# Batch 0's gate and up projections as seven block products, with the sums of the weights partly made one slot earlier

## The chip, the cores and the metric

The kernel runs on one core of a Trainium2 chip. The metric is the device time of one execution in microseconds. TensorE (PE) multiplies matrices, VectorE (DVE), ScalarE (ACT) and GpSimd (POOL) do the elementwise work, and SyncE (SP) issues most of the transfers (DMAs). Each engine works through its own list of instructions in order; an instruction that waits holds up everything behind it on that engine.

## The reference, cut to what matters

The kernel computes one transformer layer in float32 on 4 batches of 512 rows of 512 numbers, with 32 query heads, 8 key heads and 1376 columns in the feed-forward part:

```python
x = x + attention(layernorm(x), Wq, Wk, Wv, Wo)     # causal softmax, rotary embedding
h = layernorm(x)
x = x + (silu(h @ Wg.T) * (h @ Wu.T)) @ Wd.T        # Wg, Wu: 1376 x 512
```

The change concerns h @ Wg.T and h @ Wu.T of batch 0 only.

## The kernel before

**Slots.** The order of all instructions is written out by hand. After an opening (batch 0's projections) come four slots, one for each batch's attention (`slot`, L1243). A slot runs 8 groups of heads. A group has four "visits", each of which puts scores on PE (L993, L1006), their exponentials on ACT (L1094), the minima on DVE (L1039) and causal selects on POOL (L1099); a group ends with the products with the values, `averages` (L1121). The scores of a group are those of the group two further on, so they run ahead. Between the visits, `gap(n)` first takes some steps from the queue `idle` of extra POOL work (`pool_steps`, L284) and then fills PE with steps of other work in proportion to their stated costs (`fill`). Slot 0 fills with the projections of batches 1 to 3; slot 1 with the last of batch 3's projection, batch 0's output projection (`attended(0)`) and its feed-forward part; slots 2 and 3 and the tail with those of batches 1 to 3.

**Gate and up, the ordinary way.** `ordinary(0)` (L544) goes through 10 blocks of 128 columns of Wg and Wu. For each it adds up four products of a 128x128 block of weights with 512 columns of h. `load_f` fetches the weights (512 KB for a block of both matrices) two blocks ahead, in three buffers of `shared`. ACT makes a tanh (L558), DVE two multiplications (L559, L561). `edge(0)` does the last 96 columns. On the trace every product appears as 8 records, because each is issued in four strips of 32 columns of weights and each strip leaves two records.

**Gate and up, as seven.** Batches 1 to 3 use `seven` (L684). It treats a 256-column piece of Wg or Wu as 2 x 2 blocks, and h as 2 x 2 blocks, and makes the product from seven block products in place of eight, with sums of blocks before and after (a form of Strassen's method). A "unit" is one such piece: 10 units, even ones of Wg, odd ones of Wu. Its seven steps are a1, y1, y2, v1, v2, w1, w2; each is a product of a 256x128 block of weights with 256 columns, that is two products of 128x128 weights with 256 columns. ACT copies one product (L727), DVE joins them (L738, L748, L749, L757), and after an even unit come two tanh (L717) and two DVE steps (L718), after an odd one two multiplications on POOL (L721). The sums of h (`sums_of`, L682) are made once per batch on DVE.

**Sums of the weights.** The seven blocks of each unit lie in DRAM, `packed[u]`. Raw blocks are copied there in slot 0 (`copies`, L653 and L654). Four sums of blocks per unit are made by `packs(u)`: a load of 2 x 256 KB into a spare buffer (L176, half of `xnTs[1]`), four sums on POOL (`combine`, L640) and a store of 512 KB (L643). All 40 sums are made in slot 1. `load_blocks` (L675) loads the blocks of a unit one unit ahead, from `packed`, in the kinds a (128 KB), y, v and w (256 KB each); y, v and w have two buffers, a has one.

**Other transfers in slot 1.** `spilled` (L1303) stores a tile of 2816 KB (`homes[3]`, the memory of `wd_sb`) to DRAM from ACT's queue; `load_down` then loads the down weights there (2560 KB at once), and `load_rest` the last 96 columns of Wg and Wu. `timed` places these at stated points on the axis of the layer's costs. Query rows for the scores are moved by DMAs too: the minima to `lowest` (L1080), and `qa` from `lowest` (five issues, L1089 and L1091, in every group). The transposed, normalised rows of batch 0 (xn) are made partly by DVE (L314) with transfers through a `flip` buffer (L318 to DRAM, L320 back), and for two of four tiles by PE with an identity (L304); the norm's power is a step on POOL (L221), the normalising one on DVE (L226).

Of the kernel before, what the change touches and what calls it, by code (L numbers as in the profile page):

```python
# [18 lines left out]
B, T, D = 4, 512, 512  # L19
NH, NKV, DH = 32, 8, 16  # L20
FF = 1376
P = 128
NT = T // P
NK = D // P
NF = (FF + P - 1) // P
# [49 lines left out]
def preln_block_kernel(  # L75
# [13 lines left out]
    nc = tc.nc  # L89
# [74 lines left out]
    packed = [dram.tile([P, 7, 2 * P], F32, name=f"packed{u}") for u in range(whole)]  # L164
    turn = xnTs[1].rearrange("p k t -> p (k t)")
    sums = turn.rearrange("p (s k t) -> p s k t", s=4, k=2)
    spare = turn.rearrange("p (u f m) -> p u f m", u=2, f=4)
    rest_w = rope_sb[:, : 2 * NK * 96].rearrange("p (a k m) -> p a k m", a=2, k=NK)


# [4 lines left out]
    def load_w(t, src):  # L175
        nc.sync.dma_start(out=t, in_=src.rearrange("(k p) m -> p k m", p=P))  # L176
# [16 lines left out]


    rows = [const.tile([P, 2, D], F32, name=f"rows{n}") for n in range(3)] + [homes[3][:, 8:10, :]]
    ROWS = {0: (0, 1), 1: (2, 0), 2: (1, 3), 3: (2, 0)}
    xr = {(b, i): rows[ROWS[b][i // 2]][:, i % 2, :] for b in range(B) for i in range(NT)}

# [83 lines left out]
    idle = deque()  # L282

    def pool_steps(n):  # L284
        for _ in range(min(n, len(idle))):
            idle.popleft()[1]()

    def need(tag):
        while any(t == tag for t, _ in idle):
# [329 lines left out]
    def after(step):  # L619
        return 0.0, step  # L620

    def packs(u):


        w, at = (wg, wu)[u % 2], 2 * P * (u // 2)
        t = spare[:, u % 2]

        def load():
            for i in range(2):
                load_w(t[:, 2 * i : 2 * i + 2, :].rearrange("p f (k m) -> p (f k) m", k=2), w[:, at + P - P * i :][:, :P])  # L630

        def combine(n):
            a11, a12, a21, a22 = (t[:, f, :] for f in range(4))
            out_, one, two, op = (
                (a22, a21, a22, ALU.add),
                (a21, a11, a21, ALU.subtract),
                (a11, a22, a11, ALU.subtract),
                (a12, a12, a11, ALU.subtract),
            )[n]
            nc.gpsimd.tensor_tensor(out_, one, two, op)  # L640

        def store():
            nc.sync.dma_start(out=packed[u][:, 3:, :], in_=t)  # L643

        return load, combine, store
# [15 lines left out]
    places = {"v": (0, (5, 6)), "w": (1024, (2, 4)), "y": (2048, (1, 3)), "a": (3072, (0,))}  # L661

    def place(kind, v):
        start, blocks = places[kind]
        size = 2 * P * len(blocks)
        return flat[:, start + (size * (v % 2) if kind != "a" else 0) :][:, :size].rearrange(
            "p (f k m) -> p f k m", f=len(blocks), k=2
        )

    def load_blocks(kind, v):  # L670
        if v >= (B - 1) * whole:
            return
        blocks = places[kind][1]
        src = packed[v % whole][:, blocks[0] : blocks[-1] + 1 : max(blocks[-1] - blocks[0], 1), :]
        nc.sync.dma_start(out=place(kind, v).rearrange("p f k m -> p f (k m)"), in_=src)  # L675

    def sums_of(which):
        x = xnTs[0]
        b11, b12, b21, b22 = (x[:, 2 * j : 2 * j + 2, 2 * P * h : 2 * P * h + 2 * P] for j in range(2) for h in range(2))
        t1, t2, t3, t4 = (sums[:, n] for n in range(4))  # L680
        one, two, by = ((t1, b12, b11), (t2, b22, t1), (t3, b22, b12), (t4, b21, t2))[which]
        nc.vector.tensor_tensor(one, two, by, ALU.subtract)  # L682

    def seven(b, n, blocks):  # L684


        x, home = xnTs[0], homes[n]
        rights = (x[:, 0:2, 0 : 2 * P], x[:, 2:4, 0 : 2 * P], x[:, 2:4, 2 * P :], *(sums[:, s] for s in (3, 0, 1, 2)))
        once = rope_sb[:, 2 * NK * 96 : 2 * T]
        carried = deque()  # L690

# [4 lines left out]
        def product(ps, right, w):  # L696
            for k in range(2):
                product_of(ps, w[:, k, :], rights[right - 1][:, k, :], k == 0, k == 1)

        def halved(t):  # L700
            return t.rearrange("p (h t) -> p h t", h=2)

        def unit(u):
            v, a, f = (b - 1) * whole + u, u % 2, 2 * (u // 2)
            left, right = slice(0, 2 * P), slice(2 * P, T)
            out = (u_sb if a else home[:, f : f + 2, :]).rearrange("p f t -> p (f t)")
            corners = out.rearrange("p (h t) -> p h t", h=4)[:, 0:4:3, :]
            ps = {}

            def twice(t):  # L710
                return t.unsqueeze(1).broadcast_to([P, 2, 2 * P])

            def ended():
                for which in (1, 0):
                    g, t = home[:, f + which, :], u_sb[:, which, :]
                    if a == 0:
                        nc.scalar.activation(t, g, AF.Tanh, scale=0.5)  # L717
                        carried.append(lambda g=g, t=t: nc.vector.scalar_tensor_tensor(g, t, 1.0, g, ALU.add, ALU.mult))  # L718
                    else:
                        engine = nc.gpsimd if narrow[0] else nc.vector  # L720
                        engine.tensor_tensor(g, g, t, ALU.mult)  # L721

            def a1():
                load_blocks("y", v + 1)
                ps["a"] = bank()
                product(ps["a"][:, left], 1, place("a", v)[:, 0])
                nc.scalar.copy(once, ps["a"][:, left])  # L727

            def y1():
                load_blocks("v", v + 1)  # L730
                load_blocks("a", v + 1)
                ps["y"] = bank()
                product(ps["y"][:, left], 2, place("y", v)[:, 0])
                owed()

            def y2():
                product(ps["y"][:, right], 6, place("y", v)[:, 1])
                nc.vector.tensor_tensor(halved(out[:, T:]), halved(ps["y"]), twice(once), ALU.add)  # L738

            def v1():  # L740
                load_blocks("w", v + 1)
                ps["v"] = bank()
                product(ps["v"][:, left], 7, place("v", v)[:, 0])
                owed()

            def v2():
                product(ps["v"][:, right], 5, place("v", v)[:, 1])
                nc.vector.tensor_tensor(corners, halved(ps["v"]), twice(out[:, 3 * T // 2 :]), ALU.add)  # L748
                nc.vector.tensor_tensor(out[:, right], ps["v"][:, right], out[:, left], ALU.add)  # L749

            def w1():
                ps["w"] = bank()
                product(ps["w"][:, left], 4, place("w", v)[:, 0])

            def w2():
                product(ps["w"][:, right], 3, place("w", v)[:, 1])
                nc.vector.tensor_tensor(corners, halved(ps["w"]), corners, ALU.add)  # L757
                ended()

            return [(0.86, step) for step in (a1, y1, y2, v1, v2, w1, w2)]  # L760

        steps = []
        for u in range(whole):
            steps += unit(u)
            if u % 2:
                steps.append(after(lambda p=u // 2: later_sums(b, n, p, (0, 1))))
        t = [after(lambda s=s: sums_of(s)) for s in range(4)]
        ends = edge(n)
        steps[12:12] = [after(moved)]
        for cut, step in zip((44, 50, 56, 62, 66, 72), blocks):  # L770
            steps.insert(cut, after(step))
# [407 lines left out]
    begin1[1]()  # L1179
    load_w(wv_sb, wv)  # L1180
    load_columns(wq_sb, wq, P, D)
    load_w(wo_sb, wo)
    thin[0] = False
    for cost, step in turned:
        step()
# [53 lines left out]
    def slot(b, steps):  # L1239
# [19 lines left out]
        def gap(n):  # L1259
            nonlocal done, part  # L1260
            part += total * shares[n] / 8
            pool_steps((3, 2, 2, 0, 3)[n])
            done = fill(steps, part, done)

        for g in groups:
# [36 lines left out]
    def spilled():  # L1302
        nc.scalar.dma_start(out=spill, in_=homes[3])  # L1303

    def load_down():
        whole = FF // P
        load_w(wd_sb[:, :whole, :], wd[: whole * P, :])
        nc.sync.dma_start(out=wd_sb[: FF - whole * P, whole, :], in_=wd[whole * P :, :])

    def restored():  # L1310
        nc.scalar.dma_start(out=homes[1], in_=spill)
# [2 lines left out]
    early = [*rest1[16:-8], *turns, begin3, *rest2, *turned3, *rest3[:-24]]  # L1314
    for u in range(whole):
        early.insert(4 * u + 4, after(lambda u=u: copies(u)))
    slot(0, early)

    before, behind = attended(0, by_pe=(2, 3))
    tiles = list(down(0, 0))  # L1320
# [13 lines left out]
        assert not asides  # L1334
        return out_steps

    asides = []
    for u in range(whole):
        load, combine, store = packs(u)
        at = 8.2 * u + 6.0  # L1340
        asides += [(max(at - 9.9, 0.5), load), (at + 5.0, store)]
        asides += [(at + 1.0 * n, lambda n=n, combine=combine: combine(n)) for n in range(4)]
    asides += [(6.0, spilled), (34.0, load_down), (34.1, load_rest)]
    start1 = [
        before[0],
        *rest3[-24:-12],
        *before[1:],
        after(lambda: load_f(0)),
        *rest3[-12:-1],
        *behind,  # L1350
        rest3[-1],
        after(lambda: load_f(1)),
    ]
    blocks = [after(lambda kind=kind: load_blocks(kind, 0)) for kind in "ayvw"]
    layer = [*ordinary(0), *edge(0), *tiles[:5], *blocks, *tiles[5:cut]]
    slot(1, [*start1, *timed(layer, asides)])

    def split(b, n):

# [65 lines left out]
```

## Time and profile before

| | |
|---|---|
| median of 3 runs | 847.34 us (846.66 to 848.84) |
| the profiled execution | 848.06 us |
| its span in the trace | 845.8 us |
| PE busy | 822.5 us (97%) |
| DVE, ACT, POOL busy | 545.5, 231.3, 352.5 us |
| PE's granted clock | 1.0 in all 40 slices |
| slot 0, from first to last group's averages | 62.1 to 171.1 us |
| slot 1 | 191.4 to 352.7 us |
| slot 2 | 375.2 to 531.1 us |

The span is the time between the first and the last instruction that the profile shows; the execution's own time contains what lies around it. In a row of the timeline the first number is the start of the instruction in the span, the second its length, and "[1.46 <-DMA shared<-in_wg]" behind it tells how long the engine stood idle before it and what released it. A row of a window gives the busy time of each engine in that stretch.

### The profile page before, as it was taken

To read this page: it belongs to the slowest core of one execution; us is meant where nothing else is said; L and a number is where in the kernel's file an instruction comes from. 1 tells how busy PE (TensorE), PEld (TensorE's weight loads), DVE (VectorE), ACT (ScalarE), POOL (GpSimd) and SP (SyncE) were. 2 spreads that over 40 slices of the span, in tenths; PEclk is the share of its full clock that TensorE was granted. 3 is DMA by queue.
4 is the path that set the end of the run, shared out by engine and by line. 5 is a ranking of instruction groups with operands and counts; after the bars stand their busy time and mean duration, and the time that the engine had idled before them with its cause. 6 is when DMAs were issued, how large, how long until landed. Compare 5 with 4: busy or idle time off the path is not lost.

```text
span 845.8 us, 28256 instructions
## 1 busy us (share of the span) xinstructions
PE 822.5 (97%) x11980; PEld 452.2 (53%) x11980; DVE 545.5 (65%) x1601; ACT 231.3 (27%) x342; POOL 352.5 (42%) x514
## 2 busy tenths in 40 slices
PE   6999999999999999999999999999999999999998
PEld 5654444544333335333555555436655556788887
DVE  7877777778555554458677776686877633656632
ACT  1045654422232322222233232222323331011100
POOL 4575574773544344223265634532244444101130
PEclk9999999999999999999999999999999999999999
DMA  8533304003764742253344632325333534545811
GB/s 259 124 96 78 91 16 91 5 3 64 232 191 144 235 137 77 88 200 77 84 155 140 196 115 66 115 47 151 96 97 103 162 106 148 119 146 174 291 33 50
DMA packets 149517, 101.57 MB, mean 120 GB/s; under 512 B 59696, under 2 KB 137264, under 8 KB 149136
## 3 DMA queue, kind: packets, MB, share of 16 engines
q1 hardware_dynamic: 149104, 94.01, 38.3%
q10 hardware_dynamic: 288, 5.77, 1.8%
q8 instruction: 94, 1.54, 0.8%
q14 instruction: 31, 0.25, 0.1%
HBM read 78.32 MB, written 25.17 MB: 122 GB/s over the span
## 4 chain that ended last, share of the span: by engine, by line
PE 76%; DVE 12%; POOL 4%; DMA 3%; issue 2%; ACT 1%; SPq 1%; POOLq 0%; DVEq 0%; ACTq 0%
PE mm L299 38%; PE mm L296 14%; PE sc L993 12%; DVE junk L1039 6%; PE av L1121 6%; PE sc L1006 4%; PE mm L590 2%; POOL e L1099 1%; DMA shared<-packed 1%; PE mm L582 1%; DVE st L218 1%; DVE rot L358 1%; ACT e L1094 1%; POOL home L425 1%; POOL qa L978 1%
## 5 line engine op out<-in xcount | busy, mean ns | idle before, releaser
L1039 DVE CUSTOM_DVE_ANT_0 junk<-sc,mask 128x128 f32<-128x128 f32 (+3 forms) x512 | 251.2, 491 | 139.0 <-PE sc L1006 78.4
L1094 ACT ACTIVATE e<-sc 128x1024 f32<-128x1024 f32 (+1 forms) x192 | 165.5, 882 | 384.4 <-PE sc L1006 300.7
L299 PE MATMUL mm<-xnT,shared 128*32 128x256 f32 (+1 forms) x3520 | 244.2, 420 | 2.3 <-DMA shared<-in_wg 1.5
L1099 POOL TENSOR_SCALAR_AFFINE_SELECT e<-e 128x512 f32<-128x512 f32 (+2 forms) x192 | 105.7, 560 | 225.4 <-ACT e L1094 222.3
L299 PEld LDWEIGHTS mm<-xnT,shared 128*32 128x32 f32 x3520 | 116.9, 110 | 113.0 <-issue 62.8
L993 PE MATMUL sc<-home,qa 32*64 32x512 f32 (+6 forms) x2048 | 156.1, 421 | 6.5 <-DVE low L1039 3.0
L1006 PE MATMUL sc<-qa,home 32*64 32x512 f32 (+6 forms) x2048 | 152.2, 427 | 1.5 <-DVE low L1039 0.8
L993 PEld LDWEIGHTS sc<-home,qa 32*64 32x64 f32 x2048 | 66.8, 131 | 90.2 <-DVE low L1039 29.1
L1121 PE MATMUL av<-e,home 128*32 128x512 f32 (+3 forms) x1024 | 81.9, 438 | 1.8 <-POOL e L1099 1.6
L296 PE MATMUL mm<-xnT,shared 128*128 128x256 f32 x360 | 80.3, 383 | 1.0 <-DMA shared<-packed 1.0
L296 PEld LDWEIGHTS mm<-xnT,shared 128*128 128x128 f32 x360 | 68.3, 192 | 12.8 <-issue 2.2
L299 PE MATMUL mm<-wd_sb,home 128*32 128x256 f32 (+3 forms) x848 | 71.4, 470 | 0.0
L1006 PEld LDWEIGHTS sc<-qa,home 32*64 32x64 f32 x2048 | 58.8, 130 | 22.5 <-issue 8.7
L1121 PEld LDWEIGHTS av<-e,home 128*32 128x32 f32 x1024 | 30.5, 109 | 47.2 <-issue 35.0
L299 PEld LDWEIGHTS mm<-wd_sb,home 128*32 128x32 f32 (+1 forms) x848 | 28.2, 110 | 36.9 <-issue 28.2
L299 PE MATMUL mm<-wo_sb,cx 128*32 128x512 f32 x384 | 45.4, 595 | 0.0
L797 POOL TENSOR_TENSOR wd_sb<-home 128x256 f32<-128x256 f32 x15 | 11.4, 759 | 75.6 <-DVE home L721 75.3
L1039 DVE DVE_READ_ACCUMULATOR2_ANT low<- 128x1 f32 x512 | 42.4, 83 | 0.0
L221 POOL TENSOR_TENSOR rstd<-rstd,neghalf 128x1 f32<-128x1 f32 x24 | 16.0, 667 | 56.8 <-DVE rstd L220 56.7
L1145 POOL TENSOR_TENSOR inv<-us,inverse 128x256 f32<-128x256 f32 x32 | 20.9, 654 | 44.5 <-DVE inverse L1138 44.3
L359 POOL TENSOR_TENSOR rot<-rot,rope_sb 128x512 f32<-128x512 f32 x18 | 25.7, 1425 | 23.0 <-DVE rot L358 22.8
L721 POOL TENSOR_TENSOR home<-home,u 128x512 f32<-128x512 f32 x20 | 25.2, 1281 | 21.2 <-DVE u L757 21.2
(146 smaller groups left out, 855.6 us busy)
## 6 DMA issues: line engine op xcount, KB each, us to landing
shared<-packed SPq DMA_DIRECT2D x90, 256.0 KB
flip<-u SPq DMA_DIRECT2D x88, 64.0 KB
packed<-xnT SPq DMA_DIRECT2D x10, 512.0 KB
xnT<-flip SPq DMA_DIRECT2D x18, 256.0 KB
wd_sb<-differences SPq DMA_DIRECT2D x7, 640.0 KB
shared<-packed SPq DMA_DIRECT2D x30, 128.0 KB
rows<-in_x SPq DMA_DIRECT2D x14, 256.0 KB
out<-rows SPq DMA_DIRECT2D x13, 256.0 KB
```

What stands on the lines that cost most here:

```text
L296: nc.tensor.matmul(out, lhsT=lhsT, rhs=rhs, start=start, stop=stop)
L299: nc.tensor.matmul(out[c : c + 32], lhsT=lhsT[:, c : c + 32], rhs=rhs, start=start, stop=stop)
L359: put(lambda: engine.tensor_tensor(rot, rot, sin, ALU.mult))
L590: nc.tensor.matmul(ps[96:P, ts(q, P)], lhsT=rest_w[:, a, kq, 32 * q : 32 * q + 32], rhs=xnTs[0][:, kq, most:], start=kq == 0, stop=kq == N ...
L721: engine.tensor_tensor(g, g, t, ALU.mult)
L993: nc.tensor.matmul(dst[at : at + 64, :n], lhsT=qa[g][rows_of(r), q : q + 64], rhs=keys_of(g)[rows_of(r), :n], start=True, stop=True,)
L1006: nc.tensor.matmul(dst[at : at + 64, first_q:], lhsT=keys_of(g)[rows_of(r), k : k + 64], rhs=qa[g][rows_of(r), P * j + first_q :], start=True,
L1039: nc.vector.tensor_tensor_reduce(out=junk[:, :n], in0=src, in1=mask[:, T - n : T] if i else mask[:, T:], scale=-1.0, scalar=BIG, op0=ALU.a ...
L1094: nc.scalar.activation(dst, src, AF.Exp, scale=1.0 / math.sqrt(DH))
L1099: nc.gpsimd.affine_select(out=e[rows, heads, c : c + P], in_=e[rows, heads, c : c + P], compare_op=ALU.is_ge, fill=0.0, base=base, pattern ...
L1121: nc.tensor.matmul(av[32 * r : 32 * r + 32, P * j :], lhsT=v[:, j, 4 * (m // 2) + r, DH * (1 - hf) : DH * (3 - hf)], rhs=e[:, r, c : c + n ...
L1145: nc.gpsimd.tensor_tensor(us[m][:, :, hf, :], turned[0][:, :, hf, :], by, ALU.mult)
```

## The change

1. Batch 0 uses `seven(0, 0, ())` in place of `ordinary(0)`; the loads of `load_f` go. The first unit runs in another order: a1, y1, w2, y2, v1, v2, w1. Its sums of h lie in other memory (two in `rows[2]`, two in `xnTs[1]`).
2. The blocks "v" and "w" of the first unit are loaded into two free rows of `homes[0]`; all four kinds of that unit are loaded near the start of slot 1.
3. The sums of the weights are a queue (`idle`) that `gap` works off: packs 0 to 2 (12 sums) in slot 0, with the memory of the output weights `wo_sb` as buffer, and packs 3 to 9 in slot 1, with rows 6 to 9 of `homes[0]`. The loads and stores of packs stand in the same queue and are issued as soon as they come to its head. The load of the output weights moves from before the opening to behind pack 2's store.
4. The down weights are loaded as 11 pieces of 256 KB, spread over the layer, and not at once.
5. The numbers of POOL steps per gap become (1, 1, 0, 0, 0) in slot 0 and (2, 2, 1, 0, 2) in slot 1.

```diff
-    spare = turn.rearrange("p (u f m) -> p u f m", u=2, f=4)
+    sums = [sums[:, n] for n in range(4)]
+    spares = (wo_sb.rearrange("p k t -> p (k t)"), homes[0][:, 6:10, :].rearrange("p f t -> p (f t)"))
+    spares = [t.rearrange("p (u f m) -> p u f m", u=2, f=4) for t in spares]
...
     def pool_steps(n):
-        for _ in range(min(n, len(idle))):
-            idle.popleft()[1]()
+        while idle and (n > 0 or idle[0][0] == "load"):
+            tag, step = idle.popleft()
+            n -= tag != "load"
+            step()
...
     def place(kind, v):
+        if v == 0 and kind in "vw":
+            return homes[0][:, 2 + (kind == "w"), :].rearrange("p (f k m) -> p f k m", f=2, k=2)
...
-            v, a, f = (b - 1) * whole + u, u % 2, 2 * (u // 2)
+            v, a, f = b * whole + u, u % 2, 2 * (u // 2)
...
-            return [(0.86, step) for step in (a1, y1, y2, v1, v2, w1, w2)]
+            order = (a1, y1, y2, v1, v2, w1, w2) if v else (a1, y1, first_w2, y2, v1, v2, last_w1)
+            return [(0.86, step) for step in order]
...
-    load_w(wo_sb, wo)
...
-            pool_steps((3, 2, 2, 0, 3)[n])
+            pool_steps(((1, 1, 0, 0, 0), (2, 2, 1, 0, 2), *[(3, 2, 2, 0, 3)] * 2)[b][n])
...
-    def load_down():
-        whole = FF // P
-        load_w(wd_sb[:, :whole, :], wd[: whole * P, :])
-        nc.sync.dma_start(out=wd_sb[: FF - whole * P, whole, :], in_=wd[whole * P :, :])
+    def load_down(f):
+        rows_of_f = min(P, FF - f * P)
+        nc.sync.dma_start(out=wd_sb[:rows_of_f, f, :], in_=wd[f * P : f * P + rows_of_f, :])
...
+    def pack(us):
+        made = [packs(u) for u in us]
+        idle.extend(("load", load) for load, _, _ in made[:2])
+        for at, (_, combine, _) in enumerate(made):
+            for n in range(4):
+                idle.append(("sum", lambda n=n, combine=combine: combine(n)))
+                if at and n == 2:
+                    idle.append(("load", made[at - 1][2]))
+                if at and n == 3 and at + 1 < len(made):
+                    idle.append(("load", made[at + 1][0]))
+        idle.append(("sum", lambda: None))
+        idle.append(("load", made[-1][2]))
+
+    def pack_first():
+        pack(range(3))
+        idle.append(("sum", lambda: None))
+        idle.append(("load", lambda: load_w(wo_sb, wo)))
...
+    early.insert(4, after(pack_first))
+    slot(0, [*early, after(ready_out)])
...
-    asides = []
-    for u in range(whole):
-        load, combine, store = packs(u)
-        at = 8.2 * u + 6.0
-        asides += [(max(at - 9.9, 0.5), load), (at + 5.0, store)]
-        asides += [(at + 1.0 * n, lambda n=n, combine=combine: combine(n)) for n in range(4)]
-    asides += [(6.0, spilled), (34.0, load_down), (34.1, load_rest)]
+    blocks = [after(lambda kind=kind: load_blocks(kind, 0)) for kind in "ayvw"]
+    layer, first_sums = seven(0, 0, ())
     start1 = [
         before[0],
+        *blocks[:2],
+        after(lambda: pack(range(3, whole))),
         *rest3[-24:-12],
+        *blocks[2:],
         *before[1:],
-        after(lambda: load_f(0)),
-        *rest3[-12:-1],
+        *rest3[-12:-2],
         *behind,
+        rest3[-2],
+        first_sums[0],
         rest3[-1],
-        after(lambda: load_f(1)),
+        first_sums[1],
     ]
-    blocks = [after(lambda kind=kind: load_blocks(kind, 0)) for kind in "ayvw"]
-    layer = [*ordinary(0), *edge(0), *tiles[:5], *blocks, *tiles[5:cut]]
-    slot(1, [*start1, *timed(layer, asides)])
+    asides = [(6.0, spilled), (34.0, load_rest)]
+    asides += [(20.0 + 4.5 * f, lambda f=f: load_down(f)) for f in range(NF)]
+    slot(1, [*start1, *timed([*layer, *tiles[:cut]], asides)])
```

## The prediction, made before the result was known

> **What bounds the kernel now.** I read the page's busy times first, then the windows of each slot, then PE's, POOL's and SP's rows around the start of slot 1, where nearly everything changes.
>
> ```profile
> PE 822.5 (97%) x11980; PEld 452.2 (53%) x11980; DVE 545.5 (65%) x1601; ACT 231.3 (27%) x342; POOL 352.5 (42%) x514
> ```
>
> TensorE is busy for 822.5 of 845.8 us. The windows (PE, PEld, DVE, ACT, POOL busy, granted clock, DMA share, GB/s) say where it is not. The first row below lies in slot 0, the next two in slot 1, the last in slot 2:
>
> ```profile
> 62.00:126.00 64.00, 60.69 (x1146) 28.98 (x1136) 45.56 (x164) 38.44 (x67) 40.61 (x63) 1.00 0.24 62
> 191.00:239.00 48.00, 46.32 (x649) 17.94 (x641) 31.75 (x100) 12.15 (x16) 19.61 (x28) 1.00 0.56 162
> 239.00:284.00 45.00, 45.00 (x608) 15.86 (x601) 24.82 (x80) 13.27 (x17) 20.13 (x32) 1.00 0.65 190
> 420.00:463.00 43.00, 43.00 (x839) 24.70 (x836) 33.71 (x95) 12.99 (x19) 26.32 (x36) 1.00 0.46 146
> ```
>
> Slot 1 has no idle PE beyond 1.7 us in its first window, and the clock is 1.00 throughout. So each product less in slot 1 ends the kernel earlier by its whole length, and each wait that reaches PE's queue there is paid whole.
>
> **Gain 1: fewer columns on PE.** PE's rows in slot 1 (start, length):
>
> ```profile
> 205.97 3.66 PE L299 MATMUL mm<-xnT,shared 128*32 128x256 f32 x64
> 210.51 1.09 PE L304 MATMUL mm<-ident,xn 128*128 128x128 f32 x8
> 213.63 1.92 PE L299 MATMUL mm<-xnT,shared 128*32 128x512 f32 x16 [1.46 <-DMA shared<-in_wg]
> ```
>
> A product of 128x128 weights leaves 8 records. The 64 records with 256 columns are 8 products; the next work starts at 209.56, 3.59 us on, so 0.45 us each. In the chain of the end, 32 records with 512 columns (4 products) take 3.57 to 3.59 us: the same time per column. Cleared of the start of a fill (1.85 us for two, 3.57 for four), 512 columns cost 0.86 us and 256 cost 0.43. Batch 0 has 80 products of 512 now (640 records), and 10 units x 7 x 2 = 140 of 256 then: 160 halves against 140. Saved: 20 x 0.43 = **8.6 us** (9.0 with 0.45).
>
> **Gain 2.** The third row waits 1.46 us for the first ordinary weights, issued only at 208.71. Unit 0's blocks are loaded at the slot's start, some 30 us earlier: **1.5 us** more. Gains: 10.1 us.
>
> **At nothing.** DVE in slot 1 loses 20 gate and up steps (0.687 and 0.688, 13.8 us) and gets per unit 0.69 + 0.69 + 0.425 + 0.69 (24.9 in all), 10 gates of 0.762 and 4 sums (3.0): +21.7 us over 184, or 5.3 us per window of 45. That makes 30 where 24.8 stand; slot 2 runs at 33.7 in 43 with PE full. ACT: 10 copies of 0.364 and 10 of 0.622 for 10 of 0.597, 3.9 us more, against 13 busy of 45. POOL in slot 1: 12 sums of 0.731 out (8.8), 10 multiplies of 1.281 in (12.8). Cover gone, slot 2 shows the price: its PE idle, 1.8 us, is about that of slot 1 (1.9). So 0 to 1. In slot 0 the 12 sums fall into POOL's idle (23 of 64 us in the first row), at one or two a gap: 0, at most 2. The output weights' load goes from SP's start to behind pack 2's store. In the trace the four flips queued after it land 6 to 6.7 us after issue, where later ones need 2.0; but the chain goes through the next flips, at 23.6. Nothing, at best -1.
>
> **What is added: waits at the head of a queue.** The change makes three queues hold things that PE wants soon.
>
> *(a) First group of slot 1 (averages at 191.4).* Pack 3's load stands on SP behind five query rows (ending 179.9) and two block loads, so issues near 181 to 182. A pair of such loads takes 3.4 us alone (issued 251.05, complete 254.8) and up to 5.2 beside others. POOL, free at 182.5, now has two of pack 3's sums ahead of the rotations, and stands until about 185.5. Sums (1.5), rotations (2.6), a third sum (0.7) and the norm's power (0.55) then put the selects of L1099 at 191 to 193 where they ended at 190.5; averages want them near 192.3. 0 to 2 us; I take 1.2.
>
> *(b) Second group (averages at 216.4).* POOL's queue gets pack 5's first sum **ahead of** the power L221 of xn tile 3. In the trace POOL and SP do this there:
>
> ```profile
> 205.92 0.78 POOL L221 TENSOR_TENSOR rstd<-rstd,neghalf 128x1 f32<-128x1 f32 x1 [2.04 <-DVE rstd L220]
> 206.65 2.02 SPq L320 DMA_DIRECT2D xnT<-flip  x2
> 208.71 0.51 SPq L176 DMA_DIRECT2D shared<-in_wg  x1
> 209.27 1.59 SPq L176 DMA_DIRECT2D shared<-in_wu  x1
> ```
>
> Pack 5's load takes the place of the row at 208.71: behind pack 3's store, eight flips and the two L320. Landing 3.4 to 5 us on, it is there at 212.5 to 214.5. Sum 0.73, power 0.78, normalising L226 0.55: xn is ready at 214.5 to 216.5, and PE transposes it (L304) at 210.51 now. L226 also stands ahead of the next minima on DVE, so PE has nothing else. 3 to 5 us if the order holds; below that only if the load is early, so 0 to 5. I take 4.2.
>
> *(c)* DVE gets three sums (0.76 each) ahead of the next group's first minima: 0 to 1, I take 0.5.
>
> *(d) First units.* Count from the first fill after those averages (218.6 before). PE: three steps of 0.86, a visit of scores (1.0), four steps, a visit, then w1 and at **8.0** the next unit's a1. SP: minima at 0.5, pack 4's store, pack 6's load, which waits until that store has landed (stores of 512 KB: 2.6 to 3.1 us alone) so goes at 4.0 to 5.0; then the second unit's y, v and a at 5.0 to 6.5, behind 512 KB. Their latency is 2.9 to 3.2 us alone; a is there at 9.5 to 10. 0 to 2.5; I take 1.8.
>
> *(e) The spill.* It is a 2816 KB store on ACT's queue, after unit 0's two tanh: at about 10.8. SP is then at five query rows (to 9.2), a block load, pack 5's store (10.2), then waits about 3 us for its landing before pack 7's load: at 13.5. The third unit's y, v, a follow at 14.5 to 16, **behind the spill**. Now:
>
> ```profile
> 223.61 0.34 ACTq L1303 DMA_DIRECT2D spill<-wd_sb  x1
> ```
> ```profile
> 223.81 1.00 SPq L176 DMA_DIRECT2D xnT<-in_wu  x2
> 224.85 1.33 SPq L176 DMA_DIRECT2D shared<-in_wg  x1
> 226.29 5.37 SPq L176 DMA_DIRECT2D shared<-in_wu  x1
> 231.76 2.51 SPq L643 DMA_DIRECT2D packed<-xnT  x1
> ```
>
> The trace has the spill complete at 234.5, 10.9 us on, and the loads issued 0.2 to 2.7 us after it complete at 235.2, 236.1, 236.9 and 237.6: none before it. SP itself hung for 5.37 us where an issue takes 0.5. That cost PE nothing, because ordinary weights were loaded two row blocks ahead. Blocks come one unit ahead. So a lands after 10.8 + 10.9 = 21.7, with 896 KB of pack and blocks in front of or beside it: 24 to 26. PE wants it at 16.1, moved by (d) to 18: 6 to 8 us, 0 if SP is past before the spill, 9 with SP held. I take 6.5.
>
> The Trainium skill ("DMA: Bandwidth & Descriptors", Queues, rings and completion order) speaks against (e): each DMA engine takes turns between the queues that have work, a packet at a time. By that rule the blocks would share the engines with the spill and land some 3 us later than alone, not 9, and the sum would be about 5 us lower. The rows above do not show it, so the sum does without it.
>
> *Later units* run as in slot 2, whose same steps wait 0.5 us for blocks; the down weights now come as 256 KB pieces. 0 to 1.
>
> **Sum.** Waits 1.2 + 4.2 + 0.5 + 1.8 + 6.5 = 14.2; gains 10.1; net +4.1. The profiled execution took 848.06 us (span 845.8), so 852.2; the median of the three runs, 847.34, lies 0.7 lower: **851.5 us**. With every wait at its upper end (19.5): 856.7. With all at nothing: 837.2.
>
> **Rivals.**
> *A, not slower: the spill catches no block.* Place: the third unit's a, decided by whether SP issues it before about 10.8 us into that fill. For it: pack 5's store may need no wait if it starts earlier. Against: SP stands behind the minima and two landings. Price: 6.5 less, 845.0.
> *B, POOL is not held.* Pack 5's load would have to land before 205.9; against it stand eight flips and two L320 that end at 208.7. 4.2 less: 847.3.
> *C, both, and the small waits at half:* 10.1 - 1.8 = 8.3 gained, 839.0. What speaks for it is that SP is now idle for long stretches, 180 to 194 among them, and PE's stalls themselves give transfers time.
> *D, more:* POOL, held by pack 7's load, brings the selects late in the next groups too, beyond 857.5.
> *That fewer columns do not save time* has the equal rates per column against it.
>
> **Chances.** Forecast case 0.48 (847.5 to 857.5), A 0.14, B 0.10, C 0.22, D 0.06. This kernel's measurement tells about 0.3% (2.5 us) from no change. Faster: C and half of A, some of the forecast's low end, 0.30; same: B and the rest of A, 0.16; slower: 0.54. The range 839.5 to 857.5 leaves out D and about half of C. The forecast's own range is 847.5 to 857.5.
>
> **What would show it.** Right: PE waits of some microseconds before the transposes L304 with L221 late behind a sum of L640 that waits for DMA; a PE wait for shared<-packed of over 5 us in the third group of slot 1, with blocks landing after the spill; PE's busy time 8 to 9 us lower. Wrong: PE idle in slot 1 near 2 us, as now; blocks that land during the spill; or a wait in slot 0, which I priced at nothing.

## The result, and the profile after

The changed kernel takes 861.52 us (median of five runs, 856.99 to 863.50), the kernel before 848.41 (five runs, 846.66 to 851.78): 1.014 times as long, with a 95% interval of 1.010 to 1.018. It is slower, as forecast, but by 13 us and not by 4, and above the range.

Lines have moved in the changed kernel: products are L304 (L299 before), the transposes L309, POOL's sums L645, the selects L1120, block loads L682, loads of packs L178, their stores L648, the spill L1323. Its page has, in answer to the rows of before:

```profile
PE 819.3 (96%) x12460; PEld 470.9 (55%) x12460; DVE 567.0 (66%) x1635; ACT 233.6 (27%) x352; POOL 366.9 (43%) x524
```
```profile
PEclk9999999999889999999999999999999999999999
```

The profiled execution took 856.99 us (span 855.3). PE is busy only 3.2 us less, not 8.6, and idle 12.7 us more. And two slices, both in slot 1, have a granted clock under nine tenths, which no slice had before. The starts of the groups' averages place the loss: 191.6 for the first of slot 1 (191.4 before), 220.8 (216.4), 254.8 (239.7), and from then on the changed kernel gains: the first of slot 2 is at 385.9 (375.2), and the distance stays. So 15 us are lost in two groups, and 4 come back. PE's waits from 191 to 400 us (total, times, longest):

```profile
PE mm L304 <- DMA shared<-packed: 8.9, 2, 7.2
PE mm L309 <- DVE xn L229: 5.5, 1, 5.5
```

**The wait for the transposes** is the one that step (b) named. POOL and PE (start, length, idle time before):

```profile
214.20 0.72 POOL L645 TENSOR_TENSOR home<-home 128x256 f32<-128x256 f32 x1 [10.93 <-DMA home<-in_wu]
214.88 0.55 POOL L224 TENSOR_TENSOR rstd<-rstd,neghalf 128x1 f32<-128x1 f32 x1
```
```profile
216.54 1.09 PE L309 MATMUL mm<-ident,xn 128*128 128x128 f32 x4 [5.51 <-DVE xn L229]
```

POOL stands 10.93 us at pack 5's first sum, with the power L224 behind it, which took place at 205.92 before; PE pays 5.51 of it.

**The waits for blocks** are steps (d) and (e). The spill goes out between pack 5's store and pack 7's load:

```profile
235.18 0.35 ACTq L1323 DMA_DIRECT2D spill<-wd_sb  x1
```
```profile
233.84 0.70 SPq L648 DMA_DIRECT2D packed<-home  x1
238.02 1.81 SPq L178 DMA_DIRECT2D home<-in_wu  x2
239.93 12.15 SPq L682 DMA_DIRECT2D shared<-packed  x7
```
```profile
234.20 1.07 PE L304 MATMUL mm<-xnT,shared 128*32 128x256 f32 x16 [1.79 <-DMA shared<-packed]
249.76 3.64 PE L304 MATMUL mm<-xnT,shared 128*32 128x256 f32 x32 [7.15 <-DMA shared<-packed]
```

SP comes to pack 7's load at 238.02, because that waits for the store before it to land, and to the third unit's blocks at 239.93. The trace has the spill complete at 246.1 and these blocks at 248.6, 249.3 and 249.6.

**What no step named** is in the last row's length: 32 records of 256 columns are four products and take 1.9 us elsewhere; here 3.64. The windows around both waits (the third number from the right is the granted clock):

```profile
216.00:220.00 4.00, 3.46 (x36) 1.84 (x44) 3.86 (x13) 0.00 (x0) 2.90 (x4) 0.50 0.00 0
220.00:225.00 5.00, 5.00 (x98) 3.41 (x86) 4.66 (x15) 1.23 (x3) 4.79 (x8) 0.96 0.01 3
250.00:254.00 4.00, 4.00 (x48) 1.97 (x48) 0.00 (x0) 0.37 (x1) 2.99 (x3) 0.50 0.16 47
254.00:258.00 4.00, 4.00 (x80) 2.45 (x68) 2.10 (x10) 1.09 (x2) 1.49 (x3) 0.93 0.02 4
```

By the clock record of the trace, PE ran at half its clock from 213.61 to 220.44 us and from 247.75 to 254.57: the clock fell while PE waited, 2.6 and 5.1 us after it had stopped, and came back 3.9 and 4.8 us after it had started again. Half of PE's time at the half clock is 1.95 and 2.41 us.

The Trainium skill has this rule ("TensorE: Matmul & The Clock Gate", What's actually happening): the clock halves after an idle window of about 3.4 us and returns after a busy one of that length, windows that run freely. The half clock and the windows are in the traces: in all fourteen executions kept here, every recorded change of the clock lies a whole number of times 3.41 us behind the first one (above 6.83, 27.31 and 6.82 us apart, which is 2, 8 and 2 windows). How idle a window must be differs from the rule. Short of the kernel's last microseconds the clock fell 15 times in these executions. It fell at the end of every window at full clock in which PE was busy for 36% of the time or less, PE being fully idle in only five of these fourteen; of those with PE busy for 43% or more it fell in one, with 48%. It came back behind windows with 89% or more. So the place of a wait in the windows matters as much as its length: waits of 1.8, 2.6 and 3.1 us were followed by a fall, and others of 1.8, 2.0 and 3.3 were not.

### The profile page after: what moved, and what is told of

Read it like the earlier page. It is cut to its first block, busy times and chain, and to the rows that moved or that the text cites. A ratio compares the mean times of both kernels' runs of the same rounds, so it can differ in the third digit from the quotient of the medians.

```text
span 855.3 us, 29332 instructions
## 1 busy us (share of the span) xinstructions
PE 819.3 (96%) x12460; PEld 470.9 (55%) x12460; DVE 567.0 (66%) x1635; ACT 233.6 (27%) x352; POOL 366.9 (43%) x524
## 4 chain that ended last, share of the span: by engine, by line
PE 74%; DVE 12%; DMA 5%; issue 3%; POOL 3%; SPq 2%; ACT 1%; POOLq 0%; DVEq 0%; ACTq 0%
PE mm L304 35%; PE mm L301 15%; PE sc L1014 11%; DVE junk L1060 6%; PE av L1142 6%; PE sc L1027 4%; PE mm L595 2%; DMA shared<-packed 2%; POOL e L1120 1%; PE mm L587 1%; DVE rot L363 1%; DVE st L221 1%; ACT e L1115 1%; PE mm L309 1%; DMA xa<-in_x 1%
## 5 line engine op out<-in xcount | busy, mean ns | idle before, releaser
L304 PE MATMUL mm<-xnT,shared 128*32 128x256 f32 x3632 | 219.7, 384 | 9.5 <-DMA shared<-packed 9.5
L1120 POOL TENSOR_SCALAR_AFFINE_SELECT e<-e 128x512 f32<-128x512 f32 (+2 forms) x192 | 106.1, 562 | 198.5 <-ACT e L1115 195.4
L304 PEld LDWEIGHTS mm<-xnT,shared 128*32 128x32 f32 x3632 | 122.1, 110 | 97.1 <-issue 33.9
L304 PE MATMUL mm<-wd_sb,home 128*32 128x256 f32 (+3 forms) x848 | 71.2, 470 | 0.0
L728 POOL TENSOR_TENSOR home<-home,u 128x512 f32<-128x512 f32 x30 | 37.8, 1283 | 28.0 <-DVE u L775 27.9
L304 PEld LDWEIGHTS mm<-wd_sb,home 128*32 128x32 f32 (+1 forms) x848 | 28.0, 110 | 36.9 <-issue 27.6
L304 PE MATMUL mm<-wo_sb,cx 128*32 128x512 f32 x384 | 45.4, 595 | 0.0
L724 ACT ACTIVATE u<-home 128x512 f32<-128x512 f32 x40 | 23.0, 622 | 63.0 <-DVE home L775 53.8
L645 POOL TENSOR_TENSOR home<-home 128x256 f32<-128x256 f32 x28 | 21.4, 765 | 35.9 <-DMA home<-in_wu 26.5
```

The lines of the kernel that those rows point to most:

```text
L304: nc.tensor.matmul(out[c : c + 32], lhsT=lhsT[:, c : c + 32], rhs=rhs, start=start, stop=stop)
L1120: nc.gpsimd.affine_select(out=e[rows, heads, c : c + P], in_=e[rows, heads, c : c + P], compare_op=ALU.is_ge, fill=0.0, base=base, pattern ...
```

## The experiments

Theory 1: the two long waits of slot 1 are what the prediction says they are, and each is longer by the half clock behind it. The rivals: the clock falls for another reason; there is simply too much to transfer in that stretch; the waits move elsewhere when one is removed. The kernel before was measured anew beside each group of runs: 848.00 us beside the first four below, 848.25 beside those on wait (b), on blocks ahead and on five and six packs, 848.14 beside the two with a third buffer, 846.91 beside those on wait (e) and on the whole spill. A ratio is to the kernel before, with its 95% interval; between groups the ratios are the better comparison.

**The changed kernel again.**

> The changed kernel once more, unaltered, as the yardstick of the other runs of this call. Its first profile took 856.99 us, the median of five runs was 861.52. Theory 1 (two long waits in slot 1, 5.5 and 7.2 us, each followed by some 4 us at half clock): the same two waits and the same two drops of the granted clock, and a time between 857 and 864; where it is longer than 857, one of the two waits is longer by as much. Rival (the clock falls for another reason, and at other places in each execution): drops of the clock at other places than behind those waits.

Measured: 862.95 us, ratio 1.017 (1.014 to 1.020). The falls of the clock lie behind waits again, against the rival. But theory 1 had the longer time wrong: (b) and (e) are not longer (5.24 and 5.53 us), a third wait is. The profiled execution took 862.83, 5.8 more than the first, and shows what differs:

```profile
237.00 0.34 ACTq L1323 DMA_DIRECT2D spill<-wd_sb  x1
```
```profile
237.60 0.37 SPq L682 DMA_DIRECT2D shared<-packed  x1
238.34 0.93 SPq L648 DMA_DIRECT2D packed<-home  x1
247.67 0.94 SPq L178 DMA_DIRECT2D home<-in_wu  x2
```
```profile
238.72 3.41 PE L304 MATMUL mm<-xnT,shared 128*32 128x256 f32 x32 [4.61 <-DMA shared<-packed]
254.13 3.64 PE L304 MATMUL mm<-xnT,shared 128*32 128x256 f32 x32 [5.53 <-DMA shared<-packed]
```

Here the second unit's blocks took 6.6 to 6.8 us to land (4.1 to 4.3 in the first execution), so wait (d) is 4.61 us and not 1.79, and has a clock drop of its own (1.5 us, beside 1.5 behind (b) and 2.4 behind (e)). SP then comes to pack 5's store just behind the spill; it lands at 247.6, and the load that waits for it goes at 247.67, ahead of the third unit's blocks, which land at 252.9 to 254.0. Here the spill delays the store, and the store's landing holds SP; in the first execution the blocks themselves were issued during the spill. The first execution was the quick one: the forecast that the median would be 0.7 us under the profiled execution failed. Why the same loads land some 2.5 us later in one execution is open.

**Sums of pack 5 later (b alone).**

```diff
-            pool_steps(((1, 1, 0, 0, 0), (2, 2, 1, 0, 2), *[(3, 2, 2, 0, 3)] * 2)[b][n])
+            counts = (2, 1, 0, 0, 4) if g == 9 else ((1, 1, 0, 0, 0), (2, 2, 1, 0, 2), *[(3, 2, 2, 0, 3)] * 2)[b]
+            pool_steps(counts[n])
```

> Pack 5's four sums on POOL move from the gaps of the second group of slot 1 to the gap behind its averages, so that the norm's power is no longer behind a sum that waits for a DMA. Theory 1: the wait of 5.5 us before the transposes goes, and with it the half clock behind it (1.9 us): 7.4 us less than the changed kernel in the same call, with about 1 us either way; no clock drop near 214 to 220, the one behind the spill stays. Rival (the sums only move the wait, to the selects of the group or to the third unit's blocks): 0 to 3 us less. Rival (the clock has nothing to do with the wait): 5.5 less, with the clock drop still there.

Measured: 855.77 us, ratio 1.009 (1.006 to 1.012): 7.2 less, as theory 1 has it. The wait before the transposes and the drop near 214 are gone, the second averages start at 214.9 (222.1 in the repeat of the changed kernel).

**The spill in pieces (e alone).**

```diff
-    asides = [(6.0, spilled), (34.0, load_rest)]
+    asides = [(34.0, load_rest)] + [(6.0 + 2.4 * f, lambda f=f: spilled(f)) for f in range(NF)]
...
-        nc.scalar.dma_start(out=spill, in_=homes[3])
+        nc.scalar.dma_start(out=spill[:, f, :], in_=homes[3][:, f, :])
```

> The spill of 2816 KB goes as 11 pieces of 256 KB, 2.4 us apart on the axis of the layer's costs, instead of at once. Theory 1: the blocks of the third unit are no longer behind 10.9 us of transfer: the wait of 7.2 us goes to under 1, and the half clock behind it (2.4 us) too: 8.5 to 9.6 us less than the changed kernel. Rival (there is simply too much to transfer in that stretch, in whatever order): blocks late all the same, 0 to 4 us less, waits spread over several units. Rival (queues take turns at the DMA engines, so that the spill does not hold the blocks up, and the wait has SP's own order as its cause): no change.

Measured: 855.35 us, ratio 1.008 (1.006 to 1.010): 7.6 less, a little short of theory 1's 8.5 to 9.6, since a wait of 2.0 us for the third unit's blocks remains, without a drop, and that of 3.7 for the second unit's, with one.

**Both.**

> Both edits. Theory 1: the two add, 16 to 17 us less than the changed kernel, that is 7 to 8 us less than the kernel before (gains of 10.1 less the 1.8 us wait for the second unit's blocks and small ones): 840 to 842. Rival (the waits overlap, or one gives the other its slack): less than the sum of the two, 850 or so, with a new wait in slot 1 that neither alone showed.

Measured: 850.14 us, ratio 1.002 (1.001 to 1.003): 12.8 less, not 16 to 17. The clock is 1.00 throughout the profiled execution (0.993 to 1.000 in the others). The rest there is one kind of wait:

```profile
PE mm L304 <- DMA shared<-packed: 8.8, 4, 3.3
```
```profile
SPq L178 <- DMA packed<-home: 6.7, 3, 3.2
```

Two of the four waits are at units that had waited in neither run alone (1.3 and 2.8 us): with PE no longer held up, blocks loaded one unit ahead are late. In that the rival was right. SP's row names the suspect: three times, for 6.7 us in all, it stands until a pack's store has landed, with block loads behind.

**PE kept busy during wait (b)**, on top of the spill in pieces: six products of ident and wo_sb into the bank of the waiting transposes, which overwrite them.

```diff
         pt = bank()
+        for _ in range(more):
+            nc.tensor.matmul(pt, lhsT=ident, rhs=wo_sb[:, 0, :], start=True, stop=True)
...
-                transposed(xn[i], i, xnTs[0])
+                transposed(xn[i], i, xnTs[0], 6 if b == 0 and i == by_pe[-1] else 0)
```

> The kernel with the spill in pieces, and in front of the transposes that wait for POOL six extra products of 128x128 with 512 columns (5.2 us of PE work, overwritten by the transposes), so that PE is busy in most of that wait. The wait itself is as long as before, since POOL's order is unchanged. Theory 1 (the half clock is the price of PE's idling): no clock drop near 215 to 222; from the first waiting transpose to the group's averages 2.4 us instead of 4.3; 1.5 us less than the kernel with the spill in pieces alone. Rival (the clock falls for a reason other than idling, such as power or the DMA traffic): the drop stays, and the time is the same or longer.

Windows of the kernel with the spill in pieces, then of this one:

```profile
219.00:222.00 3.00, 3.00 (x31) 1.39 (x37) 2.90 (x11) 0.00 (x0) 2.54 (x3) 0.52 0.00 0
```
```profile
219.00:222.00 3.00, 2.34 (x35) 1.19 (x41) 2.90 (x11) 0.00 (x0) 2.49 (x2) 1.00 0.00 0
```

The drop is gone, so idling causes it. But the time is 855.23 us (ratio 1.010, 1.007 to 1.013) against 855.35 (1.008), no gain: the averages start at 222.7 in both, for POOL, held up as long as before, starts its selects at 222.0 in both. The half clock behind wait (b) was hidden. So the 7.2 us of the run with pack 5's sums later is the price of POOL's hold, which delays the selects as well as the transposes; theory 1 came to nearly the same figure by adding a half clock that cost nothing.

**PE kept busy during wait (e)**, on top of pack 5's sums later: eight such products in front of the third unit's first one.

> The run with pack 5's sums later (spill whole), and eight extra products of 128x128 with 512 columns (6.9 us of PE work, overwritten at once) in front of the third unit's first product, so that PE is busy in most of the wait for its blocks. The blocks land as late as before. Theory 1 (the clock falls because PE idles, and behind this wait nothing else is late, so that its price is real): no clock drop behind the wait; from the blocks' landing to the group's averages some 3 us instead of 5.3; 2 to 3 us less than that run, for which 855.8 was the median. Rival (as behind the first wait, something else is late and the half clock is hidden): no drop, and the same time. Rival (the fall has another cause): drop and time stay.

Measured: 852.85 us, ratio 1.008 (1.005 to 1.011), where the run it is built on had 855.77 and 1.009 (1.006 to 1.012): the medians differ by 2.9 us, but the ratios are too close to show a gain of the whole kernel. The profiled executions show the price. The run it is built on, then this one:

```profile
248.35 3.64 PE L304 MATMUL mm<-xnT,shared 128*32 128x256 f32 x32 [8.76 <-DMA shared<-packed]
253.65 2.56 PE L1142 MATMUL av<-e,home 128*32 128x512 f32 x32
```
```profile
239.03 7.13 PE L735 MATMUL mm<-wo_sb,ident 128*128 128x512 f32 x16
246.10 1.93 PE L304 MATMUL mm<-xnT,shared 128*32 128x256 f32 x32
248.90 2.39 PE L1145 MATMUL av<-e,home 128*32 128x512 f32 x32
```

From the first product with the blocks to the averages 2.8 us in place of 5.3: here nothing else was late, and the half clock costs its 2.5 us, which useless work in the wait saves.

**The second unit's blocks ahead of pack 6's load**: (2, 1, 0, 0, 2) for the second group, on top of both edits.

> Both edits, and the last two sums of pack 5 one gap later still, so that pack 4's store and pack 6's load stand on SP behind the second unit's y, v and a instead of ahead of them. Theory 1: the wait of 3.3 us for the second unit's blocks goes; 2.5 to 3.5 us less than with both edits, 847. Rival (one unit ahead is too short whatever the order, as every later unit has the same traffic): the wait comes at the third unit instead; 0 to 1 us less.

Measured: 849.50 us, ratio 1.001 (1.000 to 1.003). The rival was right: the wait for the second unit is gone, one of 2.96 us for the third is there, and ACT's exponentials are late once (1.8 us, with a drop).

**Five and six packs in slot 0**, on top of both edits (the buffers changed to match; with six packs the counts are 2, 1, 1, 0, 0).

```diff
-        pack(range(3))
+        pack(range(5))
...
-            counts = (2, 1, 0, 0, 4) if g == 9 else ((1, 1, 0, 0, 0), (2, 2, 1, 0, 2), *[(3, 2, 2, 0, 3)] * 2)[b]
+            counts = (2, 1, 0, 0, 4) if g == 9 else ((2, 1, 0, 0, 0), (2, 2, 1, 0, 2), *[(3, 2, 2, 0, 3)] * 2)[b]
```

> Both edits, and five packs (20 sums) instead of three (12) in slot 0, at two and one sums per gap. Theory 1: slot 1 has 2 MB less to move in its first groups, and the waits for blocks (8.8 us with both edits) fall to 4 to 6; slot 0 costs 0 to 1: 3 us less than with both edits, 847. Rival (slot 0 is bound by chains of short waits, and SP behind the stores or POOL behind the loads lengthens them): slot 0 some 2 to 4 us longer, nothing gained.

> As the run with five packs, with six (24 sums) in slot 0, at two, one and one sums per gap. Theory 1: a further 1 us less in slot 1, slot 0 the same. Rival: slot 0 longer by 2 us or more, as POOL's selects come late.

Measured: 859.00 and 858.36 us, ratio 1.013 both (1.011 to 1.015, 1.011 to 1.014). Slot 0 ends 10 and 14 us later. The rival was right, and by more than it said. In the run with six packs PE waits in slot 0 for POOL's selects for 9.2 us, 5.9 of them at once; in the changed kernel it is 0.6 us. The largest of these waits is not the length of the added sums but the hold of wait (b) again. In the run with five packs:

```profile
155.20 0.99 SPq L178 DMA_DIRECT2D wo_sb<-in_wg  x2
```
```profile
159.91 0.73 POOL L645 TENSOR_TENSOR wo_sb<-wo_sb 128x256 f32<-128x256 f32 x1 [5.79 <-DMA wo_sb<-in_wg]
```

SP came late to a pack's load, and POOL stood 5.8 us at the first sum of that pack (9.4 with six packs), with selects behind it. The 12 sums that the change put into slot 0 cost nothing, as forecast; with eight or twelve more, a sum reached the head of POOL's queue before its load had landed. How much of the rest is the added sums' own length was not tried.

**A third buffer for packs**, on top of both edits:

```diff
-        t = spares[u > 2][:, u % 2]
+        t = spares[0][:, u % 2] if u < 3 else more[(0, 1, 0, 2, 1, 0, 2)[u - 3]]
...
+    more = [spares[1][:, 1], spares[1][:, 0], turn[:, :1024].rearrange("p (f m) -> p f m", f=4)]
```

> Both edits (sums of pack 5 later, spill in pieces), and a third buffer for packs 6 and 9 (the free half of xnTs[1]), so that the load of a pack on SP no longer waits some 3 us for the landing of the store of the pack two before it. Theory 1 (the remaining 8.8 us of waits for blocks come from SP standing in those waits ahead of the block loads): SP's 6.7 us of waits for stores go, PE's waits for blocks fall to 3 to 5 us, 845 to 847, below the kernel before. Rival (the transfers themselves are what is late: packs, blocks and down weights together): SP waits elsewhere, PE's waits stay at 7 to 9, 849 to 850.

Measured: 845.70 us, ratio 0.9975 (0.9959 to 0.9991), as theory 1 has it. In the profiled execution (843.62 us) PE's waits for blocks fall from 8.8 to 0.4 us, further than the 3 to 5 expected:

```profile
PE mm L305 <- DMA shared<-packed: 0.4, 1, 0.4
```
```profile
SPq L179 <- DMA packed<-home: 0.5, 1, 0.5
```

The number of bytes is the same. So it was not too much to transfer: block loads stood on SP behind an instruction that waited.

**The same with blocks first** (the count (2, 1, 0, 0, 2)).

> The same with the last sums of pack 5 one gap later, so that the second unit's blocks stand ahead of pack 6's load. Theory 1: 0 to 2 us less than with the third buffer alone, 844 to 846, as the first of the waits goes too. Rival: the first wait goes and a later one grows by as much, no difference.

Measured: 843.29 us, ratio 0.9942 (0.9926 to 0.9957): 2.4 less, theory 1 and a little more. In the profiled execution, 840.61 us, PE waits for no block in slot 1, and is idle for 1.4 us in it.

**The same with the spill whole again.**

> The fastest version so far (sums of pack 5 later, blocks first, third buffer) with the spill whole again, at once, as in the changed kernel. Theory 1 (a transfer issued behind the spill lands behind it; what decides is whether SP is past the third unit's blocks by then): SP now issues those blocks about when the spill goes, so the wait of 7 us for them goes to 0 to 2, while blocks issued later, for the fourth unit, may wait 1 to 4: 844 to 848. Rival (the spill slows everything around it, whichever order): a wait of 5 us or more for the third unit's blocks again, with a clock drop: 850 or more. Rival (with SP free the spill costs nothing): the time of the version with pieces.

Measured: 841.98 us, ratio 0.9942 (0.9926 to 0.9958): as quick as with pieces, which is the second rival's time and better than theory 1 gave it.

```profile
224.09 3.12 SPq L683 DMA_DIRECT2D shared<-packed  x4
227.31 0.38 SPq L649 DMA_DIRECT2D packed<-home  x1
```
```profile
227.57 0.34 ACTq L1325 DMA_DIRECT2D spill<-wd_sb  x1
```

SP has issued the third unit's blocks before the spill, and the spill costs one wait of 1.4 us further on. Pack 5's store, issued at 227.31, landed only at 238.6, but with a third buffer no load stood waiting for it. That is the deciding point of rival A: what made the spill dear was SP's place when it came.

## Why the prediction was wrong

- **Gains (10.1).** Somewhat less. In slot 1 the time from each product row of L299 to the next row on PE sums to 119.4 us before and to 110.0 in the version without block waits, 9.4 less, the wait of 1.5 for the first weights included. PE's whole busy time in slot 1 fell by 7.0 us (table below), where 8.6 were forecast.
- **(a), 1.2, and (c), 0.5:** 0.2 and nothing to be seen. POOL did wait 3.0 us for pack 3's load, but the selects ended 2.2 us later and PE hardly noticed.
- **(b), 4.2:** 5.5, above the upper end of 5, by the mechanism named. Undone alone, 7.2 us: the prediction priced the late transposes and left out that the selects in front of the averages stand in the same queue of POOL.
- **(d), 1.8:** right in the first profile, 4.6 in the second, 3.7 in two experiments. The upper end, 2.5, came from landings beside little other traffic.
- **(e), 6.5:** 7.15, by the mechanism named, and 5.5 in the second profile by the case of its upper end, "SP held". SP's order decided, as rival A had it.
- **Nothing for slot 0 and the output weights:** right, 0.1 us.
- **The step that failed** is the sum: it counted each wait at its own length, "paid whole", and no more. PE's clock fell to half behind each of the two long waits, and PE lost another 1.95 and 2.41 us there, 4.4 in all, which the sum had at nothing. The first profiled execution (856.99) lies 4.8 above the 852.2 forecast for it; the other errors nearly cancel. Behind (e) the 2.4 are the price of the half clock itself; behind (b) POOL's late selects would have taken as much without it, as the run with PE kept busy there shows.
- **The clock in the trace of before.** It is printed as 1.00 throughout, but its record starts only at 12.35 us, and the transposes in front of that, behind PE's first wait, are slow. Four of them before, then four at full clock in the changed kernel (at half clock they took 1.09, above):

```profile
6.03 1.12 PE L304 MATMUL mm<-ident,xa 128*128 128x128 f32 x4 [6.03 <-DVE xa L226]
```
```profile
210.38 0.66 PE L309 MATMUL mm<-ident,xn 128*128 128x128 f32 x4
```

  So that trace already had a hint that PE is slow behind a long wait.
- **The step to the median** failed too: it took 0.7 us off the profiled execution, and 4.5 had to be added. Waits on landings vary from one execution to the next, and the first profile ((b), (d) and (e) together 14.5 us, 12.5 forecast) was the fastest of the changed kernel's nine.

Slot 1, from its first averages to those of slot 2, shows the account in us:

| | length | PE busy | PE idle |
|---|---|---|---|
| kernel before | 183.80 | 181.88 | 1.92 |
| changed, first profile | 194.30 | 178.56 | 15.74 |
| changed, second profile | 198.40 | 180.35 | 18.05 |
| third buffer and blocks first | 176.20 | 174.84 | 1.36 |

In the first profile slot 1 is 10.5 us longer: 13.8 more idle (three waits of 14.5, less the 1.5 for the first weights, and small ones) and 3.3 less busy (7.0 saved, 4.4 lost to the half clock, 0.7 unexplained). The rest of the kernel is 1 us shorter. In the second the three waits are 15.4 and the half clock behind them costs 5.4.

Undoing (e) alone gave 855.35 us, not the 845.0 of rival A, for (b) and (d) stood. With (b) and (e) both undone, as in rival C (839.0), it was 850.14; only a third buffer and blocks first brought 842 to 843.

## What to carry to other kernels

Read the order on the issuing queue, not only the bytes: a load that waits for a store's landing holds every load behind it. With a third buffer and the blocks first, cutting the spill into pieces was worth nothing. When a change makes PE wait for a few microseconds, add the half clock behind the wait (1.5 to 2.4 us here), unless another engine is late by as much anyway. And work that a busy engine's queue takes on "in its idle time" must not stand ahead of a short step that PE waits for.

## What the runs showed of the hardware

- Transfers issued on SP 2.8 to 8.2 us behind a store of 2816 KB on ACT's queue completed only after it, at 247.0 to 249.6 us where the store completed at 246.1. The rule of the Trainium skill weighed in the prediction ("DMA: Bandwidth & Descriptors", Queues, rings and completion order), that queues take turns at the DMA engines, holds in the trace and did not help the later ones. From 226 to 231 us in the kernel before, ACT's queue (q10, the spill) and SP's (q1, loads of packs and weights) moved as many packets, but the spill's are of 22 KB and the loads' of 0.5 KB:

```profile
q10 hardware_dynamic: 93, 2.10, 111.6%
q1 hardware_dynamic: 94, 0.05, 3.2%
```

  The numbers are packets, MB and share of the 16 engines. The prediction took the turns to share the bytes. In pieces, the spill's packets are of 2 KB.
- The clock changed only at the ends of windows of 3.41 us, and fell behind a window in which PE had been busy for up to 36% (once 48%): a wait of 1.8 us was followed by a fall in one run, a wait of 3.3 us in another was not.
- Executions of the changed kernel spread over 7 us, those of the kernel before over 5, and those of the version without block waits and with the spill whole over 2.
